# A two-layer gated cross-attention kernel: ten 512x512x512 products of layer 1 (queries, mixture) as seven half-size products for eight

## The chip, the cores and the metric

The kernel runs on one NeuronCore of a Trainium2 chip. The metric is the device time of one launch in microseconds (us), the median of several executions. TensorE (PE) multiplies; its weight loads (PEld) overlap its matmuls. VectorE (DVE), ScalarE (ACT) and GpSimd (POOL) do the rest; SyncE (SP) issues most DMAs, in the order of its queue.

## The reference

A token stream x of 16 batches of 128 tokens and 512 features passes two layers. Each adds a gated attention over a context and a gated feed-forward part, all in f32:

```python
x = x + tanh(g_xattn[0]) * L0_xattn(layernorm(x), ctx, ...)   # 16 heads, low-rank queries and keys
x = x + tanh(g_ffn[0])   * L0_ffn(layernorm(x), ...)          # W1, W2 with 8 low-rank experts, top 2
x = x + tanh(g_xattn[1]) * L1_xattn(layernorm(x), ctx, ...)   # 16 heads of 32, causal
x = x + tanh(g_ffn[1])   * L1_ffn(layernorm(x), ...)
# L1_xattn: qp = q @ Wq.T; k, v = split(ctx @ Wkv.T); softmax(qh kh / sqrt(32), causal) vh; @ Wout.T
# L1_ffn, a mixture of 8 low-rank maps of rank 64:
h     = relu(x @ W1 + b1)                       # 512 -> 512
alpha = softmax(h @ W2 + b2)                    # 512 -> 8
vx    = einsum('krd,bsd->bskr', V, x)           # 512 -> 8 x 64 = 512
out   = einsum('bsk,kdr,bskr->bsd', alpha, U, vx)
```

Three maps of layer 1 are 512x512 on all tokens and matter here: the queries (Wq), `hidden` (W1) and `ranks` (V).

## The kernel before

The 16 batches make four groups of 512 tokens (`GB` = 4 batches, `NG` = 4 groups). The kernel is one program written out by a Python generator; PE's matmuls and SP's DMAs keep the order in which the program emits them (`keep_in_program_order` in `matmul` and `send`), the other engines' order is a list scheduler's.

Layer 0's attention (to about 470 us) runs in steps u of two batches. Between its matmuls, `combine_next` prepares the feed-forward part's weights for products by Winograd's form of Strassen's scheme: `load_quarters` fetches four quarter blocks, `sum_quarters` makes four sums of them on POOL (L826), and `keep_quarters` stores blocks and sums to DRAM two calls later. It is called 18 times, three per step. Layer 0's feed-forward part (to about 1140 us) then takes seven half-size products for eight, with weights streamed through rings.

Layer 1's attention (to about 1420 us) is a loop over s = 2 to 17. In step s PE does `values(s-2)`, from step 4 on every fourth step `keys`, `score(s)` and `project(s-2)`. After `score(s)`, DVE, ACT and POOL make the softmax of batch s: DVE adds the mask (L1338) and takes maxima (L189), ACT makes the exponentials (L194), POOL multiplies by the reciprocals (L201), DVE transposes into `eb` (L1344); there is one `eb`. Then `carry(s)` sends it in 10 DMAs (7 on SP, 3 on POOL) to the tile that `values(s)` reads two steps later.

The remaining work of layer 1 fills this loop. `fill` is a list of units, in order: queries of groups 1 to 3, `hidden`, `share_parts`, `ranks` and `mixture` of groups 0 to 2. `plan` says for each step how many units `take` pops at four places: before `values`, after it, after `score` (there `near[0]` is set, and drains go to DVE), after `project`. A unit of `queries`, `hidden` or `ranks` is one block of 128 outputs for the group's 512 tokens: four f32 matmuls into one of two PSUM banks (`tr_tile`; the last ranks use four others), drained by one instruction. `settle` follows some places: it makes the softmax over the eight maps (`shares`), stores it to DRAM in four DMAs (`shared<-rows`) and reads it back spread over partitions in eight (`late<-shared`, the tile `avT`). Each `ranks` drain multiplies by `avT` (L1481). `ffn_normal` (L1397) and `ffn_tokens` normalise and turn a group's tokens for the mixture.

After the loop come, with nothing to interleave but each other, the ranks of group 2, the turned tokens of group 3 (`xtr_f`), its `hidden`, `share_parts`, `settle`, `store(1)` (which sends finished batches out), its `ranks`, and the last mixtures. The mixture's weights W1, V and U stay in one tile `mw_sb`, loaded in steps 3, 5 and 7.

Of the kernel before, what the change touches and what calls it, by code (L numbers as in the profile page):

```python
# [11 lines left out]
ALU = mybir.AluOpType  # L12
# [30 lines left out]
def kernel(  # L43
# [165 lines left out]
    wd = ctx.enter_context(tc.tile_pool(name="wd", bufs=1, space=bass.MemoryType.DRAM))  # L209

# [167 lines left out]
    with tc.tile_pool(name="a0", bufs=2) as ap, tc.tile_pool(name="a0s", bufs=3) as sp:  # L378
# [418 lines left out]

        def load_quarters(u):
            q = op.tile([P, 4, 2, P], F32, tag="wo", name=f"quarters_{u}")
            if u < NF // 2:  # L800
                near, far = ts(u, P), ts(u + NF // 2, P)
                for n, (half, cols) in enumerate(((0, near), (1, near), (1, far), (0, far))):
                    rows = slice(half * 2 * P, (half + 1) * 2 * P)
                    send(q[:, n], f_w1[rows, cols].rearrange("(c p) f -> p c f", p=P))
            else:
                for n in range(2):
                    rows = slice((u - NF // 2 + n * NF // 2) * P, (u - NF // 2 + n * NF // 2 + 1) * P)
                    send(
                        q[:, 2 * n : 2 * n + 2],
                        f_w2[rows].rearrange("p (h c f) -> p h c f", h=2, c=2),  # L810
                    )
            sums = op.tile([P, 4, 2, P], F32, tag="wo", name=f"sums_{u}")
            return q, sums

        def sum_quarters(u, q, sums):
            a, b, c, d = [q[:, n] for n in range(4)]
            if u < NF // 2:

                parts = ((d, c, ALU.add), (sums[:, 0], a, ALU.subtract),
                         (a, d, ALU.subtract), (b, sums[:, 1], ALU.subtract))  # L820
            else:

                parts = ((b, a, ALU.subtract), (d, sums[:, 0], ALU.subtract),
                         (d, b, ALU.subtract), (c, sums[:, 1], ALU.subtract))
# [3 lines left out]
        def keep_quarters(u, q, sums):  # L828
            if u < NF // 2:
                send(w1_kept[u][:, :3], q[:, :3])  # L830
                send(w1_kept[u][:, 3:], sums)
            else:
# [7 lines left out]
        quarters = []  # L840

        def combine_next():

            t = len(quarters)
            if 2 <= t <= NF + 1:
                keep_quarters(t - 2, *quarters[t - 2])
            quarters.append(load_quarters(t) if t < NF else None)
            if 1 <= t <= NF:
                sum_quarters(t - 1, *quarters[t - 1])
# [57 lines left out]
        for u in range(1, last + 1):  # L907
# [41 lines left out]
            soft_step(now, 2)  # L949
            gather(2 * v + 1)  # L950
# [263 lines left out]
    def turned(layer, b, xn, dst):  # L1214
        tr = (tr_tile, acc_tile)[b % 2](f"xtr_{layer}_{b}")
        for c in range(ND):
            transpose(tr[:, ts(c, P)], xn[:, ts(c, P)], ident)
        drain(
            dst.rearrange("p t (c i) j -> p c t i j", c=ND)[:, :, :, b % GB, :],
# [45 lines left out]
    def moving(tokens, d):  # L1265
        return tokens[:, :, ts(d, GB), :].rearrange("p t i j -> p t (i j)")

    def from_moving(ps):
        return ps.rearrange("p (t i j) -> p i t j", t=NK, i=GB)

    def to_batches(t):
        return t.rearrange("p (i t j) -> p i t j", i=GB, t=NK)

    def standard(xb, g, mv, rstd, layer, behind=None):

        wide = by_blocks(xb).rearrange("p k (c i) j -> p c k i j", c=ND)
        for i in range(GB):
# [6 lines left out]
                wide[:, :, :, i, :], xn.rearrange("p (c k j) -> p c k j", c=ND, k=NK)  # L1284
# [16 lines left out]

    def queries(g, c):
        q_ps = tr_tile(f"q1_ps{g}_{c}")
        for d in range(ND):
            matmul(
                q_ps, aqo_sb[:, d, ts(c, P)], moving(xa[g], d),
                start=(d == 0), stop=(d == ND - 1),
            )
        if g == 1:
            q_c = late[:, 2, 4 * c : 4 * c + 4].rearrange("p c t -> p (c t)")  # L1310
        else:
            q_c = le.tile([P, GT], F32, tag=f"q{c}", name=f"q1_{g}_{c}")
        drain(to_batches(q_c), from_moving(q_ps))
        qs.setdefault(g, []).append(q_c)
# [3 lines left out]
    def score(b):  # L1318
        g, i = divmod(b, GB)
        v_ps = tr_tile(f"v1_ps{b}")  # L1320
# [6 lines left out]
        for c in range(ND):  # L1327
            for j in range(4):
# [3 lines left out]
                    qs[g][c][rows, ts(i, P)], ks[g][c][rows, ts(i, P)],  # L1332
# [78 lines left out]
    def hidden(g, c):  # L1411
        h_ps = tr_tile(f"h1_ps{g}_{c}")
        for d in range(ND):
            matmul(
                h_ps, mw_sb[:, d, ts(c, P)], moving(xf[g], d),
                start=(d == 0), stop=(d == ND - 1),
            )
        h_c = ap.tile([P, GT], F32, tag=f"h{c}", name=f"h1_{g}_{c}", bufs=1)
        if near[0]:
            nc.vector.tensor_scalar(  # L1420
                to_batches(h_c), from_moving(h_ps), mb1_sb[:, c : c + 1], 0.0,
                ALU.add, ALU.max,
            )
        else:
            nc.scalar.activation(
                to_batches(h_c), from_moving(h_ps), AF.Relu, bias=mb1_sb[:, c : c + 1]
            )
        hs.setdefault(g, []).append(h_c)

    def share_parts(g):  # L1430
        lTs[g] = lnp.tile([P, GT], F32, tag="xn", name=f"lT_{g}")
        ps = tr_tile(f"lT_ps{g}")
        for c in range(ND):
            matmul(ps[ts(c, BK)], mw2_sb[:, c, :], hs[g][c], start=True, stop=True)
# [8 lines left out]
    def shares(g):  # L1443
# [23 lines left out]
        avT[g] = late[:, 3 - g % 2].rearrange("p (c i) t -> p c i t", c=ND)  # L1467
        for k in range(K2):
            send(
                avT[g][ts(k % 2, R2), k // 2], shared[:, k, :].partition_broadcast(R2)  # L1470
            )

    def ranks(g, c):
        v_ps = (tr_tile if g < NG - 2 else mm_tile)(f"vx_ps{g}_{c}")
        for d in range(ND):
            matmul(
                v_ps, mw_sb[:, ND + d, ts(c, P)], moving(xf[g], d),
                start=(d == 0), stop=(d == ND - 1),
            )
        part = to_batches(avT[g][:, c].rearrange("p i t -> p (i t)"))  # L1480
        nc.vector.tensor_tensor(part, from_moving(v_ps), part, ALU.mult)  # L1481

    def mixture(b):
        g, i = divmod(b, GB)
        y_ps = (acc_tile, tr_tile)[b % 2](f"my_ps{b}")
        for c in range(ND):
            matmul(
                y_ps, avT[g][:, c, i], mw_sb[:, 2 * ND + c, :],
# [5 lines left out]
    def last_mixture(b):  # L1494

        g, i = divmod(b, GB)
        for h, begin in enumerate((nc.sync, nc.scalar)):
            half = slice(h * D // 2, (h + 1) * D // 2)
            y_ps = (acc_tile, tr_tile)[h](f"my_ps{b}_{h}")[:, : D // 2]
            for c in range(ND):  # L1500
                matmul(
                    y_ps, avT[g][:, c, i], mw_sb[:, 2 * ND + c, half],
                    start=(c == 0), stop=(c == ND - 1),
                )
            dst = xt[b][:, half]
# [3 lines left out]
            begin.dma_start(out=out[b][:, half], in_=dst)  # L1509
# [10 lines left out]
    def units(what, g, ns=range(ND)):  # L1520
        return [lambda n=n: what(g, n) for n in ns]

    def mixtures(g, ns):
        return [lambda n=n: mixture(g * GB + n) for n in ns]

    def one(what, g):
        return [lambda: what(g)]

    fill = units(queries, 1) + units(queries, 2) + units(queries, 3, (0, 1))
    fill += units(hidden, 0) + units(queries, 3, (2,)) + one(share_parts, 0)  # L1530
    fill += units(queries, 3, (3,))
    for g, n in ((0, 3), (1, 4)):

        fill += units(ranks, g)
        if g == 0:
            fill += one(ffn_tokens, 1)
        fill += mixtures(g, range(n)) + units(hidden, g + 1) + one(share_parts, g + 1)
        fill += mixtures(g, range(n, GB))
    fill += units(ranks, 2)
# [6 lines left out]

    def take(n):
        for _ in range(n):
            fill.pop(0)()
# [79 lines left out]
    mw_sb = ap.tile([P, 3 * ND, D], F32, name="mw_sb", bufs=1)  # L1629
# [5 lines left out]
    for s in range(AHEAD, NB + AHEAD):  # L1635
# [38 lines left out]
        if s in (3, 5, 7):  # L1674
            n = s // 2 - 1
            send(
                mw_sb[:, n * ND : (n + 1) * ND, :],
                (m_w1, m_vT, m_uT)[n].rearrange("(c p) d -> p c d", p=P),
            )
        store(2)  # L1680
    take(4)
    g = NG - 1
    ffn_tokens(g)
    mixture((g - 1) * GB)
    for unit in units(hidden, g):
        unit()
# [5 lines left out]
    for unit in units(ranks, g):  # L1692
        unit()
# [76 lines left out]
```

## Time and profile before

| | |
|---|---|
| time, median of 3 (lowest to highest) | 1499.27 us (1497.1 to 1499.42) |
| the profiled execution's own time | 1500.14 us |
| its span, first to last instruction | 1498.3 us |
| granted TensorE clock | 0.998 |
| busy: PE, DVE, POOL, ACT | 99%, 56%, 31%, 29% |
| DMA moved | 163.5 MB, mean 109 GB/s |
| layer 1's attention and mixture | from about 1140 us to the end |

Times in the profile are us from the span's start; "busy" of PE counts matmuls whose ends are modelled. A row of the timeline has start, length, engine, line, operation, tiles and shape, the number of records merged, and in brackets the idle time before it and what ended it. All matmuls go through the helper at L169 and most DMAs through the one at L179, so groups are told apart by tile names.

### The profile page before, as it was taken

The page shows a single profiled execution, that of the slowest core. Times are in us where ns is not written, and L with a number is a line of the kernel's source. Part 1 is how long each engine was busy: PE and PEld are TensorE (multiplying, and loading weights), DVE is VectorE, ACT ScalarE, POOL GpSimd, SP SyncE. Part 2 cuts the span into 40 slices and gives each one's busy share as a digit, 9 for nine tenths or more (in the row PEclk, how much of TensorE's full clock was granted, in tenths as well). Part 3 has the DMA queues.
Part 4 walks back from the last instruction along what each step waited for, and adds up shares of the span by engine and source line. Part 5 has one row for each costly group of instructions (what it writes and reads, how often), then busy time and mean ns, then how long its engine had stood idle before and what let it go on. Part 6 is the DMA issues. An engine that isn't in the chain of part 4 may idle for free. (4 is left out here: it accounts for less than half of the span.)

```text
span 1498.3 us, 19508 instructions
## 1 busy us (share of the span) xinstructions
PE 1477.4 (99%) x6752; PEld 997.9 (67%) x6752; DVE 832.9 (56%) x1722; ACT 436.9 (29%) x1432; POOL 466.5 (31%) x500
## 2 busy tenths in 40 slices
PE   7999999999999999999999999999999999999999
PEld 5567778778877666876678666876668444444444
DVE  2274644654656555655564656455556776757422
ACT  1262432432441122012210321022203565545310
POOL 1153533623422233204320442124414333324200
PEclk9999999999999999999999999999999999999999
DMA  7533645344244822452246222721242342323212
GB/s 265 144 94 94 188 140 153 111 119 125 64 81 139 249 74 74 122 151 74 74 113 159 74 74 72 197 90 63 80 136 71 76 127 71 84 61 90 64 29 99
DMA packets 142274, 163.50 MB, mean 109 GB/s; under 512 B 54096, under 2 KB 102224, under 8 KB 140000
## 3 DMA queue, kind: packets, MB, share of 16 engines
q1 hardware_dynamic: 139024, 157.13, 36.5%
q0 software_dynamic: 2016, 4.13, 1.1%
q8 instruction: 54, 0.88, 0.3%
q10 hardware_dynamic: 1136, 0.99, 0.2%
q14 instruction: 44, 0.36, 0.1%
HBM read 106.35 MB, written 18.09 MB: 83 GB/s over the span
## 5 line engine op out<-in xcount | busy, mean ns | idle before, releaser
L1130 POOL TENSOR_TENSOR near<-base,a 128x512 f32<-128x512 f32 x32 | 42.6, 1332 | 345.0 <-ACT base L1127 233.5
L201 POOL TENSOR_TENSOR e<-e,rden_a 128x512 f32<-128x512 f32 x64 | 66.6, 1040 | 164.5 <-DVE rden_a L199 141.8
L169 PE MATMUL q_ps<-xnT_a,fq 128*128 128x256 f32 (+1 forms) x448 | 115.8, 410 | 0.0
L1127 ACT ACTIVATE a<-a 128x512 f32<-128x512 f32 x64 | 40.3, 630 | 256.8 <-DVE a L1126 256.8
L169 PE MATMUL l_ps<-t,b_sb 128*128 128x512 f32 x256 | 115.1, 592 | 0.0
L696 ACT ACTIVATE e<-s_ps,nmx_a 128x128 f32<-128x128 f32 x256 | 90.2, 386 | 78.0 <-DVE nmx_a L685 40.4
L194 ACT ACTIVATE e<-e,nmx_a 128x128 f32<-128x128 f32 x256 | 98.8, 387 | 34.7 <-DVE nmx_a L189 34.7
L1126 DVE TENSOR_TENSOR a<-l_ps,base 128x512 f32<-128x512 f32 x64 | 44.0, 688 | 108.0 <-PE l_ps L169 107.9
L169 PEld LDWEIGHTS q_ps<-xnT_a,fq 128*128 128x128 f32 x448 | 84.8, 190 | 24.5 <-issue 12.5
L703 POOL TENSOR_TENSOR e<-e,rden_a 128x512 f32<-128x512 f32 x64 | 66.0, 1039 | 100.7 <-DVE rden_a L701 100.7
L169 PEld LDWEIGHTS l_ps<-t,b_sb 128*128 128x128 f32 x256 | 48.6, 190 | 59.5 <-issue 57.6
L169 PE MATMUL fy_ps<-ring,far 128*128 128x256 f32 x384 | 87.2, 380 | 0.0
L169 PE MATMUL y_ps<-fo_raw,c 128*128 128x256 f32 x384 | 85.8, 380 | 0.9 <-DVE c L85 0.9
L776 DVE SCALAR_TENSOR_TENSOR x<-y_ps,gates,x 128x256 f32<-128x256 f32 x112 | 48.7, 477 | 67.0 <-PE y_ps L169 66.9
L1192 DVE SCALAR_TENSOR_TENSOR x<-fy_ps,gw,x 128x256 f32<-128x256 f32 x112 | 46.5, 475 | 69.3 <-PE fy_ps L169 69.3
L169 PEld LDWEIGHTS fy_ps<-ring,far 128*128 128x128 f32 x384 | 72.6, 190 | 13.6 <-issue 4.0
L169 PEld LDWEIGHTS y_ps<-fo_raw,c 128*128 128x128 f32 x384 | 72.3, 190 | 10.7 <-ACT c L87 1.0
L1344 DVE STREAM_TRANSPOSE eb<-e 128x512 f32<-128x512 f32 x64 | 45.5, 712 | 42.0 <-POOL e L201 37.4
L169 PE MATMUL ht_ps<-T,ring 128*128 128x256 f32 x256 | 65.7, 379 | 0.0
L169 PE MATMUL t_ps<-a,a_sb 128*128 128x512 f32 x128 | 65.4, 592 | 0.0
L169 PE MATMUL t_ps<-base,a_sb 128*128 128x512 f32 x128 | 65.4, 592 | 0.0
L169 PE MATMUL y_ps<-fo_sums,c 128*128 128x256 f32 x256 | 60.4, 385 | 2.1 <-ACT c L87 0.8
(257 smaller groups left out, 2956.3 us busy)
## 6 DMA issues: line engine op xcount, KB each, us to landing
ring<-w SPq DMA_DIRECT2D x32, 896.0 KB, 4.5
eT<-eb SPq DMA_DIRECT2D x312, 64.0 KB, 2.0
ring<-w SPq DMA_DIRECT2D x16, 1024.0 KB, 5.3
ring<-in_f_w SPq DMA_DIRECT2D x12, 1024.0 KB, 6.1
wq<-in_wq SPq DMA_DIRECT2D x8, 512.0 KB, 6.1
x<-in_x SPq DMA_DIRECT2D x16, 256.0 KB, 4.6
quarters<-in_f_w SPq DMA_DIRECT2D x32, 128.0 KB, 2.5
w<-sums SPq DMA_DIRECT2D x8, 512.0 KB, 3.6
```

Source lines behind the costliest of these rows:

```text
L169: ins = nc.tensor.matmul(*args, **kw)
L194: nc.scalar.activation(dst[:, ts(i, P)], src[:, ts(i, P)], AF.Exp, bias=nmx[:, i : i + 1], accum_out=den[:, i : i + 1],)
L201: nc.gpsimd.tensor_tensor(d3, d3, rden.unsqueeze(2).to_broadcast([P, 4, P]), ALU.mult)
L696: nc.scalar.activation(e[:, ts(i, P)], s_ps[:, ts(i, P)], AF.Exp, bias=nmx[:, i : i + 1], accum_out=den[:, i : i + 1],)
L703: nc.gpsimd.tensor_tensor(e3, e3, rden.unsqueeze(2).to_broadcast([P, 4, P]), ALU.mult)
L776: pin(nc.vector.scalar_tensor_tensor(dst, y_ps, gate_x[0], dst, ALU.mult, ALU.add))
L1126: nc.vector.tensor_tensor(a, l_ps, base, ALU.add)
L1127: nc.scalar.activation(a, a, AF.Gelu_apprx_tanh)
L1130: nc.gpsimd.tensor_tensor(mix, base, second, ALU.add)
L1192: nc.vector.scalar_tensor_tensor(dst, y_ps[:, ts(i, half)], q.first[:, t : t + 1], dst, ALU.mult, ALU.add,)
L1344: nc.vector.transpose(by_blocks(ebs[b])[:, :, 4 * j : 4 * j + 4, :].rearrange("p k n i -> p n k i"), e.rearrange("p (n k i) -> p n k i", n ...
```

## The change

Queries of groups 2 and 3, and `hidden` and `ranks` of all four groups, become seven products of half size (256 outputs, 256 tokens and 256 inputs, in four blocks) instead of four units; with the queries of groups 0 and 1, whose moving operand is now taken in two halves of 256 tokens, they read a group's tokens, which are now stored in an order in which each half and quarter is contiguous (`placed`, `moving`).

- Layer 0's attention: `combine_next` makes the weights' quarter sums of Wq, W1 and V too, six more units (four loads, four POOL sums, seven stores each), with one more call per step.
- Layer 1: `begin` makes four sums of a group's tokens (two on DVE, two on POOL) in what was Wq's place. `product` does one of the seven and adds its result to the others: on ACT, DVE and POOL, or on DVE alone where `near[0]` is set. The ranks' multiplication by `avT` goes to POOL (group 3: DVE), and `settle` is called in it.
- The weights come through a ring of six slots, 256 KB each: six at the end of step 2, then one after each product but the first. U has a tile of its own, loaded in step 4.
- `take` gives out work by cost: 1 for a half-size product, 2 for an old unit, 0 for sums and `share_parts`; a place is worth all costs over 48 (80/48). The fill's order changes a little.

```diff
+        def by_columns(u):
+            return u < NF // 2 or u >= NF
...
+            elif u >= NF:
+                kept_w, cols = l1_kept[(u - NF) // 2], ts(u % 2, P)
+                for n in range(7):
+                    send(kept_w[n][:, :, cols], q[:, n] if n < 3 else sums[:, n - 3])
...
+        NW = NF + 6
...
-            if 2 <= t <= NF + 1:
+            if 2 <= t <= NW + 1:
                 keep_quarters(t - 2, *quarters[t - 2])
...
             soft_step(now, 2)
+            if u < last - 1:
+                combine_next()
             gather(2 * v + 1)
...
+    def token_sums(b11, b12, b21, b22):
+        t_1, t_2, t_3, t_4 = [apart[:, n] for n in range(4)]
+        nc.vector.tensor_tensor(t_1, b12, b11, ALU.subtract)
+        nc.vector.tensor_tensor(t_2, b22, t_1, ALU.subtract)
+        nc.gpsimd.tensor_tensor(t_3, b22, b12, ALU.subtract)
+        nc.gpsimd.tensor_tensor(t_4, b21, t_2, ALU.subtract)
...
+    def fetch():
+        n = len(fetched)
+        if n == len(wanted):
+            return
+        slot = ring3[:, n % SLOTS]
+        send(slot, l1_kept[wanted[n][0]][wanted[n][1]])
+        fetched.append(slot)
...
+    def product(what, g, n, moving_of, parts, finish):
+        rhs = moving_of()
+        w = fetched[used[0]]
+        ps = tr_tile(f"{what}_ps{g}_{n}")
+        for m in range(2):
+            for c in range(2):
+                matmul(
+                    ps[:, ts(m, half)], w[:, c, ts(m, P)], rhs[n][c],
+                    start=c == 0, stop=c == 1,
+                )
+        if used[0]:
+            fetch()
+        used[0] += 1
...
+        elif n == 3:
+            if by_dve:
+                add(c12, src, parts[2], ALU.add)
+                add(c22, src, parts[3], ALU.add)
+            else:
+                nc.scalar.copy(c22, src)
+                nc.gpsimd.tensor_tensor(c12, c22, parts[2], ALU.add)
+                nc.gpsimd.tensor_tensor(c22, c22, parts[3], ALU.add)
+            finish(g, (1, 1))
...
+        order7 = (0, 1, 4, 5, 3, 2, 6)
...
+    def kept_ranks(g, quarter):
+        if quarter is None:
+            vxs[g] = ap.tile([P, ND, GT], F32, tag="h", name=f"vx_{g}", bufs=1)
+            return vxs[g]
+        settle()
+        i, j = quarter
+        a = avT[g][:, 2 * i : 2 * i + 2, ts(j, half)]
+        (nc.vector if g == NG - 1 else nc.gpsimd).tensor_tensor(
+            a, a, vxs[g][:, 2 * i : 2 * i + 2, ts(j, half)], ALU.mult
+        )
...
+    fill = units(queries, 1) + query_products(2) + query_products(3)
+    fill += hidden_products(0)
+    for g, n in ((0, 3), (1, 3)):
+        r = rank_products(g)
+        fill += (r[:1] if g == 0 else []) + one(share_parts, g)
+        fill += r[1 if g == 0 else 0 :]
         if g == 0:
             fill += one(ffn_tokens, 1)
-        fill += mixtures(g, range(n)) + units(hidden, g + 1) + one(share_parts, g + 1)
+        fill += mixtures(g, range(n)) + hidden_products(g + 1)
         fill += mixtures(g, range(n, GB))
-    fill += units(ranks, 2)
+    r = rank_products(2)
+    fill += one(share_parts, 2) + r
+    h_last, r_last = hidden_products(NG - 1), rank_products(NG - 1)
+    rate = sum(cost for cost, _ in fill) / 48
...
     def take(n):
-        for _ in range(n):
-            fill.pop(0)()
+        owed[0] += n * rate
+        while n and fill and fill[0][0] / 2 <= owed[0]:
+            cost, unit = fill.pop(0)
+            owed[0] -= cost
+            unit()
...
     settle()
     store(1)
-    for unit in units(ranks, g):
-        unit()
+    run(r_last)
```

## The prediction

> **What bounds the kernel now.** I read the page's engine line first, then the timeline of TensorE (PE) over the last layer, then the timelines of VectorE (DVE) and of the SyncE queue (SP), and last the list of waits.
>
> ```profile
> PE 1477.4 (99%) x6752; PEld 997.9 (67%) x6752; DVE 832.9 (56%) x1722; ACT 436.9 (29%) x1432; POOL 466.5 (31%) x500
> ```
>
> The timeline's columns are start and length in us, engine, line, operation, out<-in, shape, records; in brackets the engine's idle time before, and what ended it.
>
> ```profile
> 1132.42 7.07 PE L169 MATMUL fy_ps<-ring,near 128*128 128x256 f32 x32
> 1139.33 1.02 PE L169 MATMUL v_ps<-akv_sb,kv1T 128*128 128x512 f32 x2
> 1441.20 13.90 PE L169 MATMUL h_ps<-xf,mw_sb 128*128 128x512 f32 x32
> 1454.93 3.60 PE L169 MATMUL my_ps<-mw_sb,late 128*128 128x512 f32 x8
> 1458.46 1.06 PE L169 MATMUL lT_ps<-h,mw_sb 128*32 128x512 f32 x8
> 1462.99 0.95 PE L169 MATMUL l_ps<-fold_sb,lT 128*128 128x8 f32 x8
> 1463.80 13.98 PE L169 MATMUL vx_ps<-xf,mw_sb 128*128 128x512 f32 x32
> ```
>
> PE has work everywhere, so its issue rate is the price list. The ends of matmuls are modelled; I go from start to start. 32 records of 512 columns take 1454.93 - 1441.20 = 13.73 us, 0.429 each; 32 of 256 columns take 1139.33 - 1132.42 = 6.91, 0.216 each. One f32 product of a 128x128 block leaves two records: a group's `hidden` is 16 blocks and shows x32. So a unit (one output block of 512 tokens) is 8 records, 3.43 us.
>
> **Part A, PE arithmetic.** Ten products (queries of groups 2 and 3, `hidden` and `ranks` of four groups) go from 32 records of 512 to 7 x 4 x 2 = 56 of 256 columns: 13.73 to 56 x 0.216 = 12.09 us, -1.64 each, -16.4. The queries of groups 0 and 1 keep eight products but in halves: 64 x 0.216 = 13.82, +0.09 each. A = -16.2 us. One half-size product is 8 x 0.216 = 1.73 us.
>
> The Trainium skill speaks against small matmuls (Perfetto Trace Analysis, Matmuls: larger ones are more efficient), and TensorE: Matmul & The Clock Gate (Part 2, Back-to-back issue gap) puts a fixed 2.5 ns on each. The rows above show 429 against 2 x 216, a loss of 3 ns per pair, which is already in 12.09; by the page's figure 24 more records a group would cost 0.06 us, so rule and row differ by nothing that counts.
>
> So the gain is sure only as far as PE never waits. Now what waits.
>
> **Part B, layer 0's attention: weight sums.** Six more `combine_next` units: 24 loads, 24 POOL sums (0.72 us by the rows of L826, 17 us in all, beside PE), 42 stores. The calls go from 3 to 4 per step of the outer loop, each on SP and POOL.
>
> ```profile
> 387.92 10.83 SPq L179 DMA_DIRECT2D eT<-eb  x16
> 398.85 2.03 SPq L179 DMA_DIRECT2D w<-sums  x4
> 407.13 11.13 SPq L179 DMA_DIRECT2D eT<-eb  x16
> ```
>
> ```profile
> POOL sums L826 <- DMA w<-sums: 65.7, 8, 16.5
> ```
>
> The second fence is of the waits: who, for whom, total us, times, longest. SP spends 0.5 to 0.75 us per issue; 66 more are 33 to 50 us, nearly all in steps 5 and 6 (20 to 22 more issues each, in 47 us of which the two carries take 22). Queued behind them are the carries, whose tiles the gathers of the next step read. The carry of batch 12 lands at 400.2 and its gather starts at 423.0; for 13 it is 419.7 and 435.6: 16 to 23 us of cover. POOL already waits 65.7 us for such stores and PE shows about 5 us of waits in that whole stretch. B = +0.7, from 0 to 4 (no gain: nothing is removed here).
>
> **Part C, steps 3 to 6 of layer 1's attention: DVE sets the pace.** `take` now spends 80 cost units over 48 places, 1.67 each. Going through `plan`, step 3 runs one unit for two (3.45 for 6.86 us) and step 5 three half products for two units (5.18 for 6.86). PE would reach `ffn_tokens(0)` in step 6 5.0 us earlier. But:
>
> ```profile
> 1181.35 1.29 DVE L1338 SCALAR_TENSOR_TENSOR e<-s_ps,causal 128x512 f32<-128x512 f32 x2 [2.46 <-PE s_ps L169]
> 1198.38 1.25 DVE L1338 SCALAR_TENSOR_TENSOR e<-s_ps,causal 128x512 f32<-128x512 f32 x2
> 1210.08 1.25 DVE L1338 SCALAR_TENSOR_TENSOR e<-s_ps,causal 128x512 f32<-128x512 f32 x2
> 1216.61 0.71 DVE L1344 STREAM_TRANSPOSE eb<-e 128x512 f32<-128x512 f32 x1 [1.55 <-DMA eT<-eb]
> 1224.05 2.01 DVE L1397 TENSOR_SCALAR late<-x,mvf,rstdf 128x512 f32<-128x512 f32 x4
> 1224.74 2.07 PE L174 MATMUL xtr_f<-ident,late 128*128 128x128 f32 x16 [0.93 <-DVE late L1397]
> ```
>
> From 1181 to 1226 DVE never waits for PE: softmax of step 3 with `standard(3)`, softmax 4 from 1198.4, softmax 5 from 1210.1, which even waits until the carry of batch 4 has read `eb`, then the normalised tokens for which PE waits at 1224.7. An earlier PE moves this by at most the 2.46 us that DVE was idle at 1181. Against that stand eight products' DVE operations and four token sums for four drains, 8 x 0.68 = 5.4 us more; the softmax leaves holes of 0.6 us before each transpose that take most of them, so +1 to +2.5. Net DVE is 0 to 1.5 us earlier, PE's 5.0 become a wait: C = +4.3, from 2.5 to 6.5.
>
> **Part D, `share_parts`.** Before, group 0's stood alone in a place, and its logits were summed after `values` and `keys`. Now `share_parts(0)` follows half product 6 and one other (1.73 us), and needs 6's DVE addition (0.7) and two ACT relus (0.69 each, L1425) behind DVE's softmax; then `settle` follows at once and waits for the drain of `lT` (0.67). 1 + 1 us; group 1's, drained while softmax 12 begins, 0 to 3. D = +3, from 1 to 6.
>
> **Part E, steps 9 to 13.** The rank multiplications go to POOL and wait there for `late<-shared`; behind them on POOL stand the softmax's normalisations (1.04 us each, every 1.99 us, leaving 0.95), and DVE's transposes wait for those. Three additions, four multiplications and two sums per group at 1.04 to 1.33 us (rows of L201, L1130) fit holes of 0.95 only nearly. `xf[1]` is sent after the last rank product, now one place later; `hidden(1)` waited 1.3 us for it before. E = +3, from 0 to 7 (no gain, since PE's other waits there are under 0.4 us).
>
> The Trainium skill (SBUF — State Buffer, Who interferes with whom) has a DVE instruction with two SBUF inputs and a GpSimd one that reads SBUF exclude each other. L201 shows 1.04 us beside a busy DVE and 1.19 at its longest near there, so this adds little; by the rule 12 such DVE sums could cost POOL 0.69 us each, an estimate of 8 us of POOL and less of PE.
>
> **Parts F and G, the weight ring behind SP.** The ring has six slots; after half product k the weights of k + 5 are sent. So the sixth and seventh products of a group need sends issued after the group's first and second. For the rank groups 2 and 3 SP, in program order, first has `settle`:
>
> ```profile
> 1465.82 1.70 SPq L179 DMA_DIRECT2D shared<-rows  x4
> 1468.71 5.20 SPq L179 DMA_DIRECT2D late<-shared  x8
> 1473.96 3.17 SPq L179 DMA_DIRECT2D out<-x  x5
> ```
>
> Group 3's ranks start at 1463.80. SP is busy with `shared` and `late` until 1473.9, 10.1 us later, then with four of those stores (2.5), so the sends for products six and seven leave 12.6 us after the start. 256 KB land 2.3 us (`out<-x`) to 3.8 (`kv<-in_kvc`) after issue, and this queue is full: 3.6. Weights at 16.2; PE wants them at 5 x 1.73 = 8.6. G = +7.6, from 6 to 10 (the stores issued at 1475.6 and 1476.4 land only at 1482). For group 2 there are no stores: `late` ends at 1428.2, 6.1 after PE's start at 1422.1, two sends, landing at 10.3 against 8.6: F = +1.5, from 0 to 3. Elsewhere the fetches stand behind carries with a whole step to spare.
>
> **What costs nothing.** `mw_sb`'s loads go; 70 sends of 256 KB come, 5 a step at 0.6 us on SP, whose carry takes 4.3 us of a step of 13.7 or more. Each drain has 1.73 us and two banks, against 0.66 to 0.69 us of DVE or ACT. `hidden(3)`'s relus lie behind `mixture(9)` (3.43 us).
>
> **Sum.** -16.2 + 0.7 + 4.3 + 3 + 3 + 1.5 + 7.6 = +3.9 us on the profiled execution's 1500.1 (span 1498.3), which is 0.9 above the median of 1499.3. Forecast against the median: 1499.3 + 3.9 = 1503.2, rounded to 1503.0. All low ends give -16.2 + 0 + 2.5 + 1 + 0 + 0 + 6 = -6.7, all high ends -16.2 + 4 + 6.5 + 6 + 7 + 3 + 10 = +20.3.
>
> **Rivals.**
> - Faster, 1494: the ring's weights are there in time. It decides at SP's order: if the last two sends of a rank group get out before `late<-shared` (within 5 us of the group's start), F and G fall away, 1503 - 9.1 = 1494. For it: the slots are free that early. Against: the stores of batches long finished stand at 1474.0 behind `late<-shared`, so SP keeps the program's order. Or C to E come out at their low ends, 3.5 in place of 10.3: 1496. Together 0.30.
> - No change, 1499: waits and saving cancel: D and E at half, 3 less, and C at 3.5. For it: a PE that has waited once finds the next operand ready, so the waits don't add in full. 0.22.
> - Slower by much, 1511: POOL stands on `late<-shared` in the middle of softmax 9 (about 6 us), DVE's transposes and drains behind it, PE on its two banks; E goes to 7 and B to 4, +7.3. 0.13.
> - The forecast, 1503: 0.35; with the last, slower has 0.48.
>
> A measurement here can't tell less than 0.2%, 3 us, from no change. The range runs from 1490 (F and G gone, C to E low in part) to 1511: it leaves out one in ten at each end.
>
> **What would show it.** PE records of 256 columns at 0.216 in x56 groups; a PE wait of about 4 us before `xtr_f` of group 0 and of 6 to 10 us in the last rank group, ended by the DMA of the ring; DVE busy from softmax 3 to `xtr_f` as now. If the last rank group takes 12.1 us with no wait, G is wrong and the kernel is faster; if PE waits often inside `q1` and `h1` products for DVE or ACT, the drains that I put at nothing are the cost.

## Result and the profile after

The changed kernel takes 1566.9 us (1565.4 to 1570.2, four runs) beside 1499.4 of the kernel before: ratio 1.0457, interval 1.0436 to 1.0477, 67.5 us slower. The forecast was 1503.0 with a range from 1490 to 1511; the side was right, the size was not, and the measured time lies far above the range. Of the profiled run (1565.4 us, span 1563.7) the page's engine line, to be held against the first line shown above:

```profile
PE 1485.3 (95%) x7056; PEld 1067.2 (68%) x7056; DVE 871.6 (56%) x1768; ACT 446.6 (29%) x1450; POOL 542.4 (35%) x570
```

PE has 304 more records, as costed (24 for each of ten products, 32 for each of the two groups of queries in halves), and is busy for 95% instead of 99%: it waits now. Taken from the starts of the score rows (`s_ps`) in PE's timeline:

| stretch | before | after | difference |
|---|---|---|---|
| start to score(0) of layer 1 | 1123.4 us | 1143.9 us | +20.5 |
| score(0) to score(15) | 264.9 us | 290.2 us | +25.3 |
| score(15) to the end | 109.9 us | 129.5 us | +19.6 |

Nearly all of the first 20 us is lost before the last gather of layer 0's attention (it starts at 492.2 for 471.8).

**The end.** PE's timeline from the sixth product of `ranks(2)` on, the rows that answer to `h_ps` and `vx_ps` of before:

```profile
1487.56 3.38 PE L169 MATMUL vx_ps<-aqo_sb,ring 128*128 128x256 f32 x8 [3.25 <-DMA ring<-l1w]
1490.78 1.89 PE L169 MATMUL vx_ps<-xf,ring 128*128 128x256 f32 x8
...
1497.89 3.62 PE L169 MATMUL h_ps<-xf,ring 128*128 128x256 f32 x16
1501.34 7.07 PE L169 MATMUL h_ps<-aqo_sb,ring 128*128 128x256 f32 x32
1508.25 1.89 PE L169 MATMUL h_ps<-xf,ring 128*128 128x256 f32 x8
1509.98 3.60 PE L169 MATMUL my_ps<-u_sb,late 128*128 128x512 f32 x8
...
1518.85 3.70 PE L169 MATMUL vx_ps<-xf,ring 128*128 128x256 f32 x16
1522.38 5.34 PE L169 MATMUL vx_ps<-aqo_sb,ring 128*128 128x256 f32 x24
1537.15 3.75 PE L169 MATMUL vx_ps<-aqo_sb,ring 128*128 128x256 f32 x8 [9.43 <-DMA ring<-l1w]
1540.70 2.36 PE L169 MATMUL vx_ps<-xf,ring 128*128 128x256 f32 x8
```

`hidden(3)` takes 1509.98 - 1497.89 = 12.09 us with no wait, exactly part A's price. `ranks(3)` waits 9.43 us before its sixth product, `ranks(2)` 3.25 us: parts G and F. The records behind a wait are longer than their like (3.75 and 3.38 us for 1.89). SP's timeline shows what the weights stood behind:

```profile
1523.72 6.03 SPq L179 DMA_DIRECT2D late<-shared  x8
1529.79 2.32 SPq L179 DMA_DIRECT2D out<-x  x4
1532.21 1.42 SPq L179 DMA_DIRECT2D ring<-l1w  x2
```

**The loop.** The longest wait, in PE's timeline, and DVE's over the same time (softmax 15; the five DVE rows of before are of softmaxes 3 to 5):

```profile
1435.66 3.72 PE L169 MATMUL h_ps<-xf,ring 128*128 128x256 f32 x16 [0.32 <-DVE x L184]
1445.70 3.78 PE L169 MATMUL h_ps<-aqo_sb,ring 128*128 128x256 f32 x8 [6.32 <-DVE p_h L1389]
```

```profile
1436.83 1.10 DVE L1327 TENSOR_TENSOR aqo_sb<-xf 128x512 f32<-128x512 f32 x1
1437.96 0.69 DVE L1328 TENSOR_TENSOR aqo_sb<-xf,aqo_sb 128x512 f32<-128x512 f32 x1
1438.57 0.74 DVE L184 SCALAR_TENSOR_TENSOR x<-my_ps,gates,x 128x512 f32<-128x512 f32 x1
1439.23 1.28 DVE L1496 SCALAR_TENSOR_TENSOR e<-s_ps,causal 128x512 f32<-128x512 f32 x2
1440.43 1.27 DVE L189 TENSOR_REDUCE nmx_a<-e 128x4 f32<-128x512 f32 x2
1441.61 1.28 DVE L1496 SCALAR_TENSOR_TENSOR e<-s_ps,causal 128x512 f32<-128x512 f32 x2
1442.90 0.18 DVE L199 RECIPROCAL rden_a<-den_a 128x4 f32<-128x4 f32 x1
1442.99 1.25 DVE L189 TENSOR_REDUCE nmx_a<-e 128x4 f32<-128x512 f32 x2
1444.30 0.71 DVE L1502 STREAM_TRANSPOSE eb<-e 128x512 f32<-128x512 f32 x1
...
1444.99 0.66 DVE L1389 COPY p_h<-h_ps 128x512 f32<-128x512 f32 x1
```

PE does two half-size products in 3.7 us, has filled both banks at 1439.4 (1435.66 + 3.72), and stands until DVE has made the token sums, a residual and the masks and maxima of a softmax, and copies `p_h`, its first drain, at 1445. Of these 8.2 us on DVE (1436.83 to 1444.99) the token sums, which are new too, are 1.7. The same kind of row stands at 1222.45 (3.23 us, `p_q`), 1270.41 (3.04), 1366.12 (1.78) and elsewhere. A unit of before gave 3.43 us to each bank, so two banks kept PE at work for 6.9 us; a half-size product gives 1.73, and two banks last 3.5.

**Layer 0.** From the lists of waits over its attention, first of before, then of after:

```profile
DVE eb L709 <- POOL e L703: 19.6, 20, 2.7
```

```profile
POOL sums L836 <- DMA w<-sums: 67.3, 10, 16.0
DVE eb L713 <- POOL e L707: 53.7, 26, 7.9
```

POOL waits for stores a little longer than before (67.3 us for these and 4.8 for the new ones, beside 65.7). What has grown most is DVE's wait for POOL's softmax multiplications, 53.7 for 19.6 us. At the first long stop, in the timelines of POOL, DVE and PE of the changed kernel:

```profile
219.91 1.04 POOL L707 TENSOR_TENSOR e<-e,rden_a 128x512 f32<-128x512 f32 x1
224.25 1.40 POOL L836 TENSOR_TENSOR sums<-quarters 128x256 f32<-128x256 f32 x2 [3.29 <-DMA w<-sums]
225.61 0.73 POOL L836 TENSOR_TENSOR sums<-sums,quarters 128x256 f32<-128x256 f32 x1
226.29 1.04 POOL L707 TENSOR_TENSOR e<-e,rden_a 128x512 f32<-128x512 f32 x1
```

```profile
227.36 0.71 DVE L713 STREAM_TRANSPOSE eb<-e 128x512 f32<-128x512 f32 x1 [5.21 <-POOL e L707]
228.00 1.25 DVE L85 COPY c<-c_ps 128x512 f32<-128x512 f32 x2
```

```profile
228.80 6.42 PE L169 MATMUL y_ps<-fo_sums,c 128*128 128x256 f32 x16 [4.68 <-DVE c L85]
```

A group of weight sums stands between two multiplications of one softmax. DVE, whose transposes are pinned in program order, waits 5.21 us for the second; behind that transpose stand the copies of a gather, and PE waits 4.68 us for those. The carries that the prediction looked at are not late: in the same list PE has no wait for `eT`.

### The profile page after: what moved, and what is told of

The parts are those of the page before. It is cut to its first block, busy times and chain, and to the rows that moved or that the text cites. A ratio compares the mean times of both kernels' runs of the same rounds, so it can differ in the third digit from the quotient of the medians.

```text
span 1563.7 us, 20570 instructions
## 1 busy us (share of the span) xinstructions
PE 1485.3 (95%) x7056; PEld 1067.2 (68%) x7056; DVE 871.6 (56%) x1768; ACT 446.6 (29%) x1450; POOL 542.4 (35%) x570
## 5 line engine op out<-in xcount | busy, mean ns | idle before, releaser
L201 POOL TENSOR_TENSOR e<-e,rden_a 128x512 f32<-128x512 f32 x64 | 67.5, 1055 | 131.0 <-DVE rden_a L199 127.2
L169 PEld LDWEIGHTS fy_ps<-ring,far 128*128 128x128 f32 x384 | 72.6, 190 | 13.6 <-issue 3.9
L169 PE MATMUL y_ps<-fo_sums,c 128*128 128x256 f32 x256 | 65.5, 412 | 15.8 <-DVE c L85 7.7
L169 PEld LDWEIGHTS y_ps<-fo_raw,c 128*128 128x128 f32 x384 | 72.3, 190 | 10.7 <-ACT c L87 1.0
L169 PEld LDWEIGHTS y_ps<-fo_sums,c 128*128 128x128 f32 x256 | 51.6, 207 | 32.4 <-issue 21.9
L836 POOL TENSOR_TENSOR sums<-quarters 128x256 f32<-128x256 f32 x44 | 31.4, 736 | 100.9 <-DMA w<-sums 67.3
L169 PE MATMUL ht_ps<-T,ring 128*128 128x256 f32 x256 | 65.7, 379 | 0.0
```

The lines of the kernel that those rows point to most:

```text
L169: ins = nc.tensor.matmul(*args, **kw)
L201: nc.gpsimd.tensor_tensor(d3, d3, rden.unsqueeze(2).to_broadcast([P, 4, P]), ALU.mult)
L836: nc.gpsimd.tensor_tensor(sums[:, n], x0, x1, what)
```

## Experiments

My theory after the traces: the loss is three separate things, sums in layer 0 (some 20 us), drains and shares in the loop (25 and the gain that is gone), the ring at the end (some 13). "As e2" and the like name the kernel that an edit starts from.

**e1: the sums alone.** The kernel before with `l1_kept`, six more units and the added call, nothing of layer 1.

> The kernel before with nothing added but layer 0's six more weight sums and their fourth call per step; layer 1 is untouched and reads none of them. My term B says +0.7 us, 1500. The reading of the two traces says that layer 0's attention ends 20.4 us later (last gather at 492.2 for 471.8): POOL stands on the stores of the sums in the middle of a softmax, DVE's transposes behind it, and the gathers' drains behind those; then this kernel takes 1519 to 1520, a third of the whole loss. A rival is that the 20 us come from DMA traffic that ends late and are made up by the feed-forward part: 1500 to 1505.

1523.7 us, ratio 1.0164 (1.0147 to 1.0181): 24.0 us, some more than the 20.5 of the changed kernel's first stretch. The feed-forward part makes nothing up.

**e2: layer 1 alone.** The changed kernel without the six units. The ring takes raw blocks of the weights instead, of the same size, so the values are others; that holds for e3 to e6, e8, e10 and e12 too:

```diff
-        send(slot, l1_kept[wanted[n][0]][wanted[n][1]])
+        w, i = wanted[n]
+        rows, cols = ts(i % 2, 2 * P), ts(i // 2 % 2, 2 * P)
+        send(slot, (a_wqT, m_w1, m_vT)[w][rows, cols].rearrange("(c p) f -> p c f", p=P))
```

> The changed kernel without layer 0's six more sums: the ring is filled with raw quarter blocks of Wq, W1 and V (256 KB each, as before, from the inputs), so the seven products don't use the summed weights. All of layer 1's work is as in the changed kernel. If the two parts add, 1566.9 - 20.4 = 1546.5, with layer 1's loop from score(0) to score(15) 25 us longer than before and the rest after it 20 us longer. My terms A and C to G say 1502.3. A rival: the late start of layer 1 costs something of its own, then under 1540.

1541.3 us, 1.0279 (1.0259 to 1.0299): 41.6 us. With e1 that makes 65.6 of 67.5: the parts add. The four times of e2 lie between 1537.4 and 1544.8 us, so a difference of 4 us against it says little.

**e3: the ring ahead.** The last two weights of `ranks(2)` and `ranks(3)` go to two `e` tiles, which the softmax has left, and are sent before `settle` (the lines that send them early; `fetch` puts them in the tiles):

```diff
+        if used[0] in (49, 63):
+            fetch()
+            fetch()
```

> As e2, but the weights of the last two products of ranks(2) and ranks(3) go to two tiles of their own and are sent two products earlier, ahead of settle's twelve DMAs. Terms F and G are these waits; the changed kernel's trace shows 3.4 and 9.6 us of PE waits on them, and PE's granted clock falls to 0.91 and 0.78 behind them. Theory: 13 us of waits and some 4 us of slower clock go, 16 to 17 us below e2. My terms said 9.1. Rival: the multiplications by late<-shared stand right behind the weights, so that only 3 to 6 us go.

1527.9 us, 1.0189 (1.0174 to 1.0204): 13.3 us below e2, less than the 16 to 17 expected and more than the 9.1 of the terms. In e2 the two waits were 1.75 and 9.03 us. PE's timeline of e3 has `ranks(3)` in 12.2 us with no wait, and no new wait behind it:

```profile
1493.01 3.70 PE L169 MATMUL vx_ps<-xf,ring 128*128 128x256 f32 x16
1496.55 5.34 PE L169 MATMUL vx_ps<-aqo_sb,ring 128*128 128x256 f32 x24
1501.73 1.89 PE L169 MATMUL vx_ps<-aqo_sb,w 128*128 128x256 f32 x8
1503.46 1.89 PE L169 MATMUL vx_ps<-xf,w 128*128 128x256 f32 x8
1505.18 17.35 PE L169 MATMUL my_ps<-u_sb,late 128*128 128x512 f32 x48
```

**e4: more banks.** `ps = (tr_tile if near[0] else mm_tile)(...)` in `product`.

> As e2, but half-size products outside the place behind score (that is, all whose drains may go to ACT) use the four PSUM banks of the scores instead of the two that they shared. If PE's waits in layer 1's loop come from two banks being too few for a product every 1.73 us, those at drains outside that place go: of 25 us some 6 to 10. Rival: they come from the place behind score, where DVE is in the softmax for 5 us before the first drain, and from settle's chain; then it is within 3 us of e2.

1541.8 us, 1.0280 (1.0265 to 1.0296): no change against e2, as the rival had it. Behind `score` the products kept their two banks, and the longest wait there stayed (4.63 us for `p_h`, 4.56 in e2). Of the others, several have moved: in PE's timeline of e4 they stand before the scores, which need those banks next and wait for the same drains:

```profile
1206.94 0.61 PE L169 MATMUL s_ps<-k,late 32*128 32x128 f32 x2 [3.77 <-DVE u_q L1398]
...
1311.78 2.07 PE L169 MATMUL s_ps<-k,q 32*128 32x128 f32 x26 [5.30 <-DVE vx L1413]
```

So lending the scores' banks doesn't help: PE still waits for the time at which DVE gets to a drain. Banks that the products have to themselves were not tried.

**e5: four drains a group.** Three of the seven results are dropped, and with them all the additions (the lines that change):

```diff
+        quarter = {1: c11, 3: c22, 2: c21, 6: c12}.get(n) if n else None
+        if n in (1, 3) and not by_dve:
+            nc.scalar.copy(quarter, src)
+        elif quarter is not None:
+            nc.vector.tensor_copy(quarter, src)
```

> As e2, but of the seven products of a group only four are drained, each by one copy, as the four units of before were; the sums with the other three are left out. PE's matmuls, weights, token sums and places stay. In e2's trace PE waits 24 us in layer 1's loop for a PSUM bank of a half-size product (longest 4.7 and 3.4 us, each for DVE's first drain behind a softmax). If the drains are what I wrongly put at nothing, 15 to 22 us go: 1519 to 1526. Rival: the softmax on DVE sets the pace whatever the drains do (my term C): then at most 6 us go, 1535.

1520.3 us, 1.0143 (1.0126 to 1.0160): 20.9 us below e2, the largest term of the loop. PE's waits between 1160 and 1440 us fall from 31.8 us in e2 to 18.6, and those for `p_q`, `p_h` and `u_q` are gone. e5 takes drains from DVE and ACT and additions from POOL in one, so how much is the banks' shorter reach and how much the work itself isn't told apart.

**e6: the shares later.** `fill += r[:3] + one(share_parts, g) + r[3:]`.

> As e2, but share_parts of groups 0 to 2 comes after three products of the ranks instead of one or none. Term D put its waits at 3 us; e2's trace shows 3.9 us for ACT's relus, 1.4 for the drain of lT and 3.7 for l_ps of group 1. If these waits are what it costs, 5 to 9 us go: 1532 to 1536. Rival: the chain from the logits to late<-shared is what the rank products wait for, and moving it later only moves the wait there: no change, or some us longer.

1551.7 us, 1.0351 (1.0335 to 1.0366): 10.4 us longer than e2; my theory's gain did not come and the rival was right. PE's timeline of e6 shows the mixture waiting for the rank multiplications in place of `lT_ps` for the relus:

```profile
1313.83 3.78 PE L169 MATMUL my_ps<-u_sb,late 128*128 128x512 f32 x4 [4.35 <-POOL late L1454]
...
1477.59 3.38 PE L169 MATMUL my_ps<-u_sb,late 128*128 128x512 f32 x4 [5.87 <-POOL late L1454]
```

**e8: the ranks' multiplications on DVE**, in place of POOL.

> As e2, but the ranks' multiplications by late are on DVE for all groups, as in the kernel before, not on POOL. Term E (3 us, 0 to 7) says that POOL stands on late<-shared in the middle of softmaxes: then 2 to 6 us go. Rival: DVE stands on it instead, with the product drains and the softmax's masks behind it, and it is 2 to 10 us longer.

1545.5 us, 1.0308 (1.0293 to 1.0324): 4.2 us above e2's median, within what e2's own times spread. The expected gain of 2 to 6 us did not come; that POOL was the better place isn't shown.

**e10: e3 and e5 in one.**

> e3 and e5 in one: weights of the last two rank products sent ahead, and only four drains a group (the sums with the other three products are left out). If the two costs are separate, 1541.2 - 13.3 - 20.9 = 1507. If PE's earlier arrival turns into another wait, 1512 to 1520.

1507.1 us, 1.0057 (1.0043 to 1.0071), as the sum of the two gains has it: the two costs are separate.

**e12: the shares free.** As e10; `share_parts` of groups 0 to 2 takes the tokens and stands before the last two products of `hidden`.

> As e10, but share_parts of groups 0 to 2 reads the tokens in place of hidden's outputs (so the shares are others) and stands before the last two products of hidden: it then waits for no relu, and its drain and settle have two products beside them. In e10's trace PE waits 4.3 us for ACT's relus before lT_ps, 1.4 and 3.7 us for the drain of lT before l_ps, and some 4 us of shorter ones right behind, for which term D has 3. If they go, 8 to 12 us do: 1495 to 1499, with term D some 10 us and not 3. Rival: what stands behind them (the rank multiplications, values) waits for the softmax's DVE then: under 4 us, 1503 or more.

1498.0 us, 0.9991 (0.9982 to 1.0001): 9.1 us below e10. The chain from `hidden` to the logits costs three times what term D had; one wait of 3.58 us before an `l_ps` is even left in e12. In the changed kernel's PE timeline it is this:

```profile
1305.30 2.39 PE L169 MATMUL lT_ps<-h,mw_sb 128*32 128x512 f32 x8 [3.78 <-ACT h L1443]
1308.49 1.88 PE L169 MATMUL l_ps<-fold_sb,lT 128*128 128x8 f32 x8 [0.79 <-DVE lT L85]
1310.21 2.05 PE L169 MATMUL v_ps<-akv_sb,kv1T 128*128 128x512 f32 x2
1312.20 2.09 PE L169 MATMUL s_ps<-k,q 32*128 32x128 f32 x32
```

The four rows take about twice what their like take elsewhere (1.06, 0.95, 1.02 and 1.17 us), at a granted clock of 0.50 from 1306 to 1316 us. Group 1's `l_ps` waits 3.49 us more, at 1388.01.

**e11: one wait and nothing else**, in the kernel before: V is loaded a second time behind `settle`.

```diff
     settle()
+    send(mw_sb[:, ND : 2 * ND, :], m_vT.rearrange("(c p) d -> p c d", p=P))
     store(1)
```

> The kernel before with one wait of PE and nothing else: V (1 MB) is loaded a second time behind settle's DMAs, and ranks(3) waits for it, about 16 us. If a wait costs only its length, the time rises by the idle time that the trace shows before vx_ps. If the clock behind it is slower, as the windows of the changed kernel show (0.78 and 0.88 in the 10 us behind waits of 5 us), it rises by 2 to 4 us more, and the records of vx_ps there are longer than 0.43 us.

1519.3 us, 1.0136 (1.0120 to 1.0151): 20.5 us. PE's timeline has 18.62 us of waiting and 15.91 for records that took 13.98, 1.93 more, together 20.55. The windows of the same kernel give PE's busy time, then PEld, DVE, ACT, POOL, and the granted clock in the third column from the end:

```profile
1482.42 15.91 PE L169 MATMUL vx_ps<-xf,mw_sb 128*128 128x512 f32 x32 [18.62 <-DMA mw_sb<-in_m_vT]
```

```profile
1480.00:1490.00 10.00, 7.58 (x13) 3.37 (x14) 0.69 (x1) 0.00 (x0) 0.00 (x0) 0.68 0.37 143
1490.00:1500.00 10.00, 10.00 (x25) 4.48 (x24) 2.07 (x3) 0.00 (x0) 0.00 (x0) 1.00 0.01 2
```

**Term B taken apart.** e1 and six more kernels, all the kernel before with the six units; each takes away or moves one suspect.

> As e1, but the fourth call per step stands beside the third at the step's end, not in the middle of the second softmax's first half. In e1 POOL reaches the sums there in front of the softmax's last two multiplications, waits up to 18 us for stores that SP issues late, DVE's transposes (pinned) wait behind POOL, the gathers' copies behind those, and PE stops 5 to 9 us three times. If the place is the cost, this is back to within 5 us of before, 1499 to 1505. Rival: it is the load on SP and the DMA queues (66 more issues), wherever they stand: 1515 to 1523.

> As e1 (layer 0's six more sums alone, four calls per step), but the stores of all 24 units are issued by POOL right behind its sums, not by SP two calls later, behind the carries. Nothing then makes POOL wait for a store that is still queued on SP. If POOL's standing on those stores, in front of the softmax's multiplications, is what costs 24 us, most goes: 1499 to 1507, and POOL's waits for w<-sums and l1w<-sums (71.5 and 28.1 us in e1) nearly vanish. Rival: the 66 more transfers or POOL's own work (17 us of sums) cost it: still 1515 or more; POOL then pays for 90 issues besides.

> As e1, but the added call makes no sums (its unit's stores send the raw blocks again, so some weights of the feed-forward part are wrong, at equal shapes and addresses): its four loads and its stores stay on SP at the same place, and only POOL has nothing to do there. e13 took the stores' wait away and left POOL with the sums and the issues, at the same 24 to 27 us; so what counts should be POOL's time in front of the softmax's multiplications, be it spent working or waiting. Then this is within 6 us of before: 1499 to 1505. Rival: 66 more DMAs on SP, with carries and loads late behind them: 1512 or more.

> As e14, but each of the six added units is stored by two DMAs in place of seven (the same bytes, as W1's units are stored), so SP issues 30 fewer, some 19 us at 0.63 us each, most of them between 352 and 395 us, where e14's last loads for the sums stand behind them and POOL waits 4.4 us in front of a softmax. If SP's backlog is the other half of term B, 4 to 8 us go: 1506 to 1510; the wait at 220 us, which comes before the first of these units, stays. Rival: what is left in e14 is not SP's issue time but the loads and stores themselves: within 2 us of e14.

> As e7 (all six units, the fourth call at the step's end), but POOL's multiplications, sums and pair sums keep the program's order, so that no group of sums stands between two multiplications of one softmax, as one did at 223 us in e1, e7, e13, e14 and e15; three groups then stand ahead of the even softmax. If that place is what costs, 6 to 12 us of e7's 13.5 go: 1501 to 1507. Rival: three groups in a row keep POOL 15 us and the whole softmax comes late: 1510 or more.

> As e16, but the fourth call stands behind pair_sums, so that two groups of sums are ahead of each softmax. If both the place between the multiplications and the crowd ahead of the even softmax count, this is the cheapest of the placements: 1499 to 1503. Rival: the group ahead of the odd softmax, which has 20 us less of cover before its gather, costs as much there: 1508 or more.

The edits: e7 `range(0 if u >= last - 1 else 2 if u > 1 else 3)` at the step's end in place of the added call; e13 `nc.gpsimd.dma_start` in `keep_quarters`, called right behind `sum_quarters`; e14 `combine_next(on_pool=False)` for the added call, which leaves its sums out and stores raw blocks; e15 is e14 with `l1_kept` laid out by unit, two stores for seven; e16 and e17 `pin(...)` around POOL's multiplications, sums and pair sums, with the added call at the step's end as in e7 (e16) or behind the pair sums (e17). Beside each, from its list of waits over layer 0's attention (150 to 500 us), DVE's wait for POOL's multiplications (`eb <- e`) and all of PE's own waits:

| kernel | us | ratio (interval) | `eb <- e`, us | PE, us |
|---|---|---|---|---|
| before | 1498.4 to 1499.6 beside these | | 19.6 | 3.8 |
| e15 two stores, no POOL in the call | 1512.7 | 1.0093 (1.0076 to 1.0110) | 28.8 | 11.7 |
| e14 no POOL in the call | 1513.9 | 1.0100 (1.0083 to 1.0117) | 35.7 | 12.4 |
| e7 call at the end | 1513.0 | 1.0086 (1.0068 to 1.0105) | 36.7 | 13.5 |
| e1 | 1523.7 | 1.0164 (1.0147 to 1.0181) | 56.2 | 20.5 |
| e13 stores by POOL | 1526.1 | 1.0181 (1.0164 to 1.0198) | 64.5 | 21.8 |
| e17 pinned, even | 1521.4 | 1.0153 (1.0138 to 1.0168) | 68.9 | 19.2 |
| e16 pinned, at the end | 1548.6 | 1.0333 (1.0316 to 1.0351) | 95.2 | 41.4 |

No single suspect carries the 24 us, and my expectations for all six failed: the times of e13 to e17 are those of the rivals, that of e7 lies between the two. Without the added call's sums (e14) 9.8 of the 24 us go, and with the call at the step's end (e7) 10.7. Late stores alone (e13) are not it, 30 issues fewer on SP (e15 beside e14) change nothing beyond the noise, and keeping the multiplications of a softmax together (e17) brings nothing either, with three groups in a row (e16) it is worse.

The time does not follow DVE's wait for POOL in proportion: e15 has 13.6 us for 9.2 more of it, e17 23.0 for 49.3. It follows PE's own waits, 1.3 to 1.7 us for each us of them, the records behind a wait being slower too. In e14 and e15 two stops make most of these waits, 5.17 and 3.47 us, and 4.96 and 3.38; the first is the stop shown above under "Layer 0", with POOL at the sums of the other calls. That POOL's place in front of the softmax makes them is shown by the rows at that stop and argued for the others. POOL's timeline of e16 shows what a group costs POOL there:

```profile
228.85 0.73 POOL L837 TENSOR_TENSOR sums<-quarters 128x256 f32<-128x256 f32 x1 [3.64 <-DMA w<-sums]
...
235.47 0.72 POOL L837 TENSOR_TENSOR sums<-quarters 128x256 f32<-128x256 f32 x1 [3.71 <-DMA w<-sums]
```

With three tiles for blocks and sums, each call's sums wait for the store of the call before: calls in a row cost POOL 6.6 us each, 2.9 of work and 3.7 of waiting, and the softmax that stands behind them is late by that. A placement that costs nothing was not found; more tiles were not tried.

**e9: the version from this.** Half-size products only for `ranks(2)`, `hidden(3)` and `ranks(3)`, where no softmax stands on DVE; the sums of V and W1 made by POOL in steps 15 and 16 from `mw_sb` (in part):

```diff
+        if s == 15:
+            t = le.tile([P, ND, GT], F32, tag="q", name="v_sums")
+            weight_sums(2, ND, [t[:, c] for c in range(ND)])
+        if s == 16:
+            weight_sums(1, 0, [
+                le.tile([P, GT], F32, tag=f"k{c}", name=f"w1_sums{c}", bufs=1) for c in range(ND)
+            ])
```

> The half-size products only where no softmax stands on DVE: ranks(2), hidden(3) and ranks(3), after the loop. All else as units of before, in halves of 256 tokens (+0.09 us each for eight groups). The four sums of V and of W1 are made by POOL in steps 15 and 16 from the weights that are in SBUF anyway, into tiles that the loop has left, so that layer 0's part has no more work and no ring is needed. e3 shows these groups at 12.1 us with no wait, for 13.8: 3 x 1.64 - 8 x 0.09 = 4.2 us less than before, 1495.1, ratio 0.9972. Rival: DVE's drains (0.69 us for 1.73 us of PE) or the token sums hold PE here too: 1498 or more.

1496.3 us beside 1498.8, ratio 0.9981 (0.9972 to 0.9990): 2.5 us faster than the kernel before, where 4.2 were expected. `ranks(2)` has a wait of 0.68 us for `u_vx` in it, `my_ps` 0.23 behind it; the rest I have not traced.

## Why the prediction was wrong, by its steps

**Part A** (-16.2) was right: 12.1 to 12.2 us a group in the changed kernel, in e3 and in e9, where nothing waits.

**Part B** (0.7; 24.0 measured) failed at the step "16 to 23 us of cover". The cover of the carries' tiles is there, and irrelevant. The softmax's multiplications stand behind the sums on POOL, DVE's transposes are pinned behind those, and the gathers' copies stand behind the transposes. I counted POOL's 17 us of sums "beside PE" and never asked what stands behind each group on POOL. The last rival had that chain (POOL standing, DVE's transposes and drains behind it, PE on its banks), but in softmax 9 of layer 1, at 7 us.

**"What costs nothing"** (0; 20.9 measured in e5) failed at "each drain has 1.73 us and two banks, against 0.66 to 0.69 us". That compares how long a drain takes with how long PE takes. What it leaves out is how long DVE may be away: two banks lasted 6.9 us before, 3.5 now, and DVE is away 5.7 us at a softmax's start: of the softmax that starts at 1198.38 under part C I showed one row, and the next drain on DVE in that timeline is at 1204.11. The last sentence of the prediction named the case; it belonged in the sum. The 20.9 also hold the additions' own time on DVE and POOL.

**Part C** (4.3) saw DVE as the pace in steps 3 to 6, which holds in part (busy for 19.0 of the 20 us from 1200, for 15.5 of the next 20), but looked for the wait before `xtr_f`. It is 1.11 us there; PE waits 8.8 us in all from 1200 to 1251, most of it before the queries' products. In e5 4.2 us are left in these steps, near C's size but at other places; C was not measured by itself.

**Part D** (3; 9.1 in e12) had the right places and the wrong sizes: 3.78 for 1 us before `lT_ps`, 3.49 for group 1's drain of `lT`, and behind the first a clock at half.

**Part E** (3): POOL waits 6.0 us in all for `late<-shared`, twice, and PE 1.4 us for POOL. No run measures it by itself; e8, with DVE in POOL's place, is not told apart from e2.

**Parts F and G** (9.1; 13.3 in e3): the mechanism, the place and the order on SP were as forecast. The term was too small: the waits were 3.25 for 1.5 and 9.43 for 7.6 us (eight `late` issues took 6.03 for 5.20, the weights landed 4.8 for 3.6 us behind their issue), and slower records came on top.

**The sum.** -16.2 + 24.0 + 20.9 + 13.3 + 9.1 = 51.1 of the 67.5. In e12, with all of these taken away, PE's timeline still has 11.3 us of waits from 1165 to 1300 us (3.58 before an `l_ps`, 1.5 to 1.6 before each of three products and one `values`); that is most of the rest, and stays without an experiment of its own. 4.3 of the 11.3 us are in steps 3 to 6, where part C had them. The new `take` by cost is in all kernels with the ring and was not run by itself. The range was too narrow because each term's high end came from its own row, and none allowed for one engine held up behind another: even all high ends together gave 1499.3 + 20.3 = 1519.6. That the side was right is in part luck, as the two largest costs stood in the sum at 0.7 and at nothing.

## What to carry to other kernels

When a step is cut into smaller pieces, cost its drains by the longest time that the draining engine stays away, against the time for which the banks last, not by busy times. When work is put on an engine that "has time", list what stands behind it there and who is pinned behind that: here six units with 17 us of sums cost 24. Products of this kind paid 2.5 us where no softmax needs the draining engine (e9); over all of layer 1 their extra drains and additions took 20.9 (e5), more than the 16.2 that the products save.

## What the runs showed of the hardware

A wait of PE can cost more than its length. In e11 18.62 us of waiting came with 1.93 us of slower records, at a granted clock of 0.68 in the ten microseconds around; in two-microsecond windows it is 0.50 up to 1486, some 4 us of work behind the wait, then 0.92 and 1.00.

The length of a short wait does not tell whether this happens. In the changed kernel the records behind 3.04 and 3.23 us have their usual length (1.99 us for eight; 4.00 for sixteen that take 3.72 elsewhere), those behind 3.25, 3.78, 6.32 and 9.43 us take up to twice theirs (3.38, 2.39 for 1.06, 3.78 and 3.75). But 2.73 us in layer 0 of the same kernel were enough (at 288.00: 5.48 us for sixteen, clock 0.74 and 0.50), and in e3 the waits of 3.04 and 3.23 us at the same two places were too (at 1248.15: 3.78 us for eight, clock 0.50; at 1200.21: 5.11 for sixteen).

It can also last longer than in e11: behind the 3.78 us of the changed kernel the clock stays at 0.50 from 1306 to 1316 us, and the five rows there take 5.3 us more than their like (`lT_ps` to `s_ps` above, then a `vx_ps` of 3.03 for 1.89), more than the wait itself.

The Trainium skill has this gate (TensorE: Matmul & The Clock Gate, Part 1): the array falls to half its clock after an idle window of about 3.4 us and comes back after about as long of sustained work; the window runs freely. By the page a return costs about 1.7 us, an estimate (half of 3.4); e11's 1.93 agrees. The shorter waits above, which were enough, and the ten microseconds from 1306 do not fit these lengths, and there the rows decide (the ends of matmuls are modelled, so a wait's length is itself not exact). Beside parts F and G, such a price would have come on top of the waits: in the changed kernel the records there take 3.8 us more than their like.
